# State sums behind the first third's side work, and out_proj two slots later: one change to a two-layer Mamba and expert kernel

## The chip, the cores and the metric

The kernel runs on one core of one Trainium2 chip. A core has a tensor engine (TensorE, PE in the profile), a vector engine (VectorE, DVE), a scalar engine (ScalarE, ACT), a general engine (GpSimd, POOL) and SyncE (SP), which issues most of the DMAs. Each engine has a queue of its own; an instruction waits on semaphores for the results of others. The metric is the time of one execution on the device in microseconds.

## What is computed

The input x is 8 images of 384 channels and 32 x 32 points, 1024 tokens per image. Layer 0 is a Mamba block with an MLP behind it, layer 1 a mixture of four experts with two chosen; both are preceded by a group norm and added to their input. Cut to what matters:

```python
x = x + L0(group_norm(x))
x = x + L1(group_norm(x))

# L0, per image, t = 1024 tokens of 384 channels, layer-normed
xm, z = split(t @ in_proj_w.T)                     # 768 channels each
xc = silu(conv3(xm) + conv_b)
dt, Bm, Cm = split(xc @ x_proj_w.T, [24, 40])
dt = softplus(dt @ dt_proj_w.T + dt_proj_b)
dA = exp(dt * A)                                   # 768 channels x 16 states
h = dA * h + (dt * xc) * Bm                        # scan over the 1024 tokens
y = (sum over states of h * Cm + xc * D) * silu(z)
t = gelu((y @ out_proj_w.T) @ mlp_w1.T + mlp_b1) @ mlp_w2.T + mlp_b2

# L1, per token
coef = weights of the two best of 4 experts
out = sum over e of coef_e * (relu(x @ w1_e.T + b1_e) @ w2_e.T + b2_e)
```

Everything is 32-bit floating point.

## The kernel before

An image is worked in two halves of 512 tokens, so there are 16 halves i. A half has 768 inner channels, six blocks d of 128, and each block has 16 states per channel, done as four groups s of four. A *round* r is one (i, d, s): 24 rounds per half, 384 in all (line 922 on). The 24 rounds of a half are called a block below, counted k = 0 to 23.

A round works on 128 partitions (32 channels x 4 states for each j of four quarters, j = 0 to 3). Its instructions are:

- `drive(r)` (L742, POOL): du = (dt x) times B, 128 x 2048, into one of three buffers du
- `decay(r, j)` (L734, ACT): exp(dt A) for one quarter; quarters 0 and 1 into the PSUM tile da_A, quarters 2 and 3 one after the other into the PSUM tile da_B
- `scan(r, j)` (L750, DVE): the recurrence over 512 tokens, four per round
- `read_out` (L754): h times C, for quarters 0 and 1 on DVE, for 2 and 3 on POOL, both into du
- `sum_states(r)` (L776, PE): four matmuls with the 0/1 matrix `sel` that add the four states into the PSUM tile y of (i, d). It reads what both read_outs wrote, and when it is done du is free for drive(r + 3).
- once in four rounds, when a d is complete, `finish` (L783, DVE): xc = y times silu(z), the gate product; it waits for the last sums of its d. `seed` (L769, ACT) then starts y of the next d with xc times D.

All other work of layer 0 and the first half of the expert layer is *side work*: in_proj for the next half (g_in, L295), x_proj (g_x), the step sizes dt (`delta`: g_dt on PE L396, three activations on ACT L400 to L402, one operation on DVE L404, one on POOL L407, then DMAs that bring dt and dt x back repeated as dtr and dxr), out_proj (g_out, L456), the MLP (hid, L478, and acc, L517), the norms, and the experts' first product (e_hid, L619, results to HBM in r_dram). It is written as generators that yield the engine wanted next, a cost and a number of slots to wait. Three times per round, `side` counts a slot, gives each engine credit (PE 2.7 per slot) and issues ready steps in order of rank while there is credit. This happens while the program is built: the result is a fixed order on each engine. The PE results of side work go to four PSUM banks and are evicted by ACT or DVE in a later slot; the expert lane has the last rank, so it takes what the others leave.

The loop of a round (L922 to L959), in the order in which it is written: `plan`, `sum_states(r - 1)`, `scan(r, 2)`, `drive(r + 1)`, `decay(r, 3)`, side work of the first third, `scan(r, 0)`, `scan(r, 3)`, side work of the second third, `decay(r + 1, 2)`, `scan(r, 1)`, the two read_outs, `decay(r + 1, 0)` and `(r + 1, 1)`, `finish` and `seed` where s = 0, side work of the last third.

out_proj(i) (L445) waits until (i, 5) is in `finished`, which `finish` sets at the end of round k = 0 of the next half, before that round's last side work. It then makes three groups of two times three matmuls; its weights (and those of all lanes) come through rings of three buffers, loaded by SP two ahead. The hidden lane of half i waits for it.

After the loop, what is left of the side work is drained, the routing weights are made, and `experts` runs the second expert product (acc, L1026) over all tokens.

Of the kernel before, what the change touches and what calls it, by code (L numbers as in the profile page):

```python
# [112 lines left out]
def layer0(ctx, tc, io, ident, cmean, eps, dram, x1_dram, gn1, logits, r_dram, group_norm):  # L113
# [77 lines left out]
    def exp_ln_tables():  # L191
        S.preload_act_table_set(EXP_LN_SET)
# [4 lines left out]
    def bank(name):  # L197
        held[0] += 1
        return ps_g.tile([P, T], F32, name=name, tag="g")
# [31 lines left out]
    def statistics(b):  # L231
        st = p2.tile([P, NH * J, 6], F32, name="st")
        for k in range(NH):
            for j in range(J):
                if b == 0:
                    part = xt[k][:, j, :]
                else:
                    yield "-", 0, 3
                    part = pst.tile([P, T], F32, name="part")
                    nc.sync.dma_start(part, chunk_of(io["x"], b * NH + k)[:, j, :])  # L240
                    yield "-", 0, 3
                yield "DVE", 0.7, 0
                V.bn_stats(st[:, k * J + j, :], part)
        g = wp.tile([P, 2], F32, name=f"gn{b}")
        yield from group_norm(st, bank, free, p2, g)

        yield "bank", 0.2, 2
        small = bank("shift")
        PE.matmul(small[:, 0:1], lhsT=cmean, rhs=g[:, 1:2], start=True, stop=True)
        yield "ACT", 0.6, 2  # L250
        mean_w = p1.tile([P, P], F32, name="mean_w")
        S.activation(mean_w, cmean, AF.Identity, scale=g[:, 0:1])
        S.activation(g[:, 1:2], small[:, 0:1], AF.Identity, bias=g[:, 1:2], scale=-float(J))
        free()
        gn[b] = g, mean_w
# [68 lines left out]
    def gate(i, d):  # L324
        while i not in normal or not w_in.turn("in_proj", ND + d):
            yield "-", 0, 1
        yield "bank", 3, 0
        g = in_proj(i, ND + d)
        yield "ACT", 0.6, 2
        z = pz.tile([P, T], F32, name="z")  # L330
        S.copy(z, g)
        free()
        gates[i, d] = z
# [40 lines left out]
    def load_b(i, s):  # L374
        bt[i, s] = load_rows("b", i, s)

    def load_c(i, s):
        ct[i, s] = load_rows("c", i, NS + s)
# [61 lines left out]
    def evict(g, wait, cost, engine, then):  # L440
        yield engine, cost, wait
        then(g)
        free()

    def out_proj(i):  # L445
        while (i, ND - 1) not in finished or i - 1 in tt:
            yield "-", 0, 1
        t = p1.tile([P, J, T], F32, name="tt")
        for j in range(J):
            g = None  # L450
            for k in range(2):
                yield "bank" if k == 0 else "PE", 3, 0
                w = w_out.take("out_proj", 2 * j + k)
                g = bank("g_out") if k == 0 else g
                for d in range(3):
                    PE.matmul(g, lhsT=w[:, d, :], rhs=xc[i, 3 * k + d], start=(k + d == 0), stop=(k == 1 and d == 2))  # L456

            def then(g, j=j):
                S.copy(t[:, j, :], g)
                ready.setdefault(i, []).append(j)  # L460
            begin(evict(g, 2, 0.6, "ACT", then), rank=1)
        out_done.add(i)
        while len(ready.get(i, [])) < J:
            yield "-", 0, 1
        tt[i] = t
# [73 lines left out]
    def out_lane():  # L539
        for i in range(NCH):  # L540
            yield from out_proj(i)
# [13 lines left out]
    def in_order():  # L555
        for n in range(NCH):
            if n > 0:
                yield from (ND + d for d in range(3, 6))
            yield from range(ND)
            yield from (ND + d for d in range(3))  # L560
        yield from (ND + d for d in range(3, 6))
# [161 lines left out]
    def at(r):  # L723
        i, k = divmod(r, per)
        return i, *divmod(k, NG)
# [18 lines left out]
    def scan(r, j):  # L744

        i, d, s = at(r)
        a = da[r, "A"][:, j, :] if j < 2 else da[r, "B"]
        b = du[r][:, j, :]
        start = 0.0 if i % NH == 0 else carry[:, d, j, s:s + 1]
        V.tensor_tensor_scan(a if j < 2 else b, a, b, start, ALU.mult, ALU.add)  # L750
# [20 lines left out]
    def sum_states(r):  # L771
        i, d, s = at(r)
        y, h = yp[i, d], du.pop(r)
        m = P // Q
        for j in range(Q):
            PE.matmul(y[j * m:(j + 1) * m, :], lhsT=sel, rhs=h[:, j, :], start=False, stop=(s == NG - 1),  # L776
                      tile_position=(0, j * m), skip_group_check=True)
# [23 lines left out]
    def begin(*new, rank=2):  # L801
        tasks.extend(Task(t, rank) for t in new)
# [59 lines left out]
    def drain(until=lambda: not tasks):  # L862
        while not until():
            credit.update(PE=99, ACT=99, DVE=99, batch=99)
            issue(everything)
            slot[0] += 1
        credit.update(PE=0, ACT=0, DVE=0)

    with tc.manual_schedule():
        w_in = Stream(pw_in, [("in_proj", k) for k in in_order()])  # L870
        begin(statistics(0))
        drain()
        begin(norm(0))
        drain()
        S.preload_act_table_set(SILU_SET)
        begin(*(conv(0, d, at_once=True) for d in range(ND)), x_proj(0))
        drain(lambda: len(xc) == ND)
        exp_ln_tables()
        drain()
        load_b(0, 0)  # L880
        load_c(0, 0)
        begin(delta(0, 0))
        drain()
        for s in range(1, NG):
            load_b(0, s)
            load_c(0, s)
        begin(delta(0, 1), rank=0)
        begin(*(gate(0, d) for d in range(3)))
        begin(silus(zs, gates, [(0, d) for d in range(3)]))
        begin(norm(1))  # L890
        w_out = Stream(pw_out, [("out_proj", k) for i in range(NCH) for k in range(2 * J)])
        w_1 = Stream(pw_1, [("mlp_w1", u) for i in range(NCH) for u in range(NF)])
        w_2 = Stream(pw_2, [("mlp_w2", 4 * j + 2 * half + k) for i in range(NCH) for half in range(2)
                            for j in range(J) for k in range(2)])
        seed(0, 0)
        w_e = Stream(pw_e, [("e_w1", u) for i in range(NCH) for u in range(E * J)])
        drive(0)
        for j in (2, 0, 1):
            decay(0, j)
        begin(out_lane(), rank=1.5)  # L900
        begin(hidden_lane(), rank=3)
        begin(second_lane(), rank=2.5)
        begin(expert_lane(), rank=4)

        batched = [False]

        def side(*engines, act=None):
            slot[0] += 1
            credit["PE"] = min(credit["PE"] + PE_SLOT, 4)
            credit["DVE"] = min(credit["DVE"] + DVE_SLOT, 2)  # L910
            if act is not None:
                credit["ACT"] = act + min(credit["ACT"], 0)
            issue({e: ENOUGH[e] for e in engines})

        def batch():

            ready = [t for t in tasks if t.engine == "batch" and t.ready <= slot[0]]
            batched[0] = bool(ready) and not batched[0]
            if batched[0]:
                min(ready, key=Task.urgency).resume()  # L920

        for r in range(rounds):  # L922
            i, d, s = at(r)
            k = r % per
            more = r + 1 < rounds
            plan(i, k)
            if r > 0:
                sum_states(r - 1)
            scan(r, 2)
            if more:  # L930
                drive(r + 1)
            decay(r, 3)
            batch()
            act = () if batched[0] else ("ACT",)
            side("PE", "DVE", *act, act=ACT_FIRST)
            scan(r, 0)
            scan(r, 3)
            last_token(G.tensor_copy, r, BB, du[r][:, BB, :])
            side("PE", *act)
            if more:  # L940
                decay(r + 1, 2)
            scan(r, 1)
            read_out(V, r, A, da[r, "A"])
            last_token(V.tensor_copy, r, A, da[r, "A"])
            read_out(G, r, BB, du[r][:, BB, :])
            if more:
                decay(r + 1, 0)
                decay(r + 1, 1)
            if s == 0 and r > 0:
                finish(*at(r - 1)[:2])  # L950
                seed(i, d)
            side("PE", "DVE", "ACT", act=ACT_LAST)
        sum_states(rounds - 1)
        finish(NCH - 1, ND - 1)
        begin(last_x1(), route(), rank=0)
        drain()
# [116 lines left out]
```

## Time and profile before

| | us |
|---|---|
| median of 3 runs | 4095.63 (4087.91 to 4099.21) |
| the profiled execution | 4110.87 |
| its span, first to last instruction | 4109.0 |
| first read_out to last read_out of the rounds | 3325 (82 to 3407) |
| from the end of the rounds to the end | about 690 |
| mean granted TensorE clock | 0.948 |
| blocks of 24 rounds from 670 us on | 210 to 214 each |
| blocks of 24 rounds before that | 192 to 199 each |

The page gives, for each group of instructions, its line, engine, operation, the tiles written and read, the shapes and the count; behind the first bar the time busy in us and the mean of one in ns; behind the second bar how long the engine sat idle just before these instructions, and who ended most of that. "PEld" are weight loads. A view by stretch lists for each stretch its length, then the busy time and number of instructions on PE, PEld, DVE, ACT and POOL, then the granted TensorE clock as a share of full speed, the busy share of the DMA engines, and GB/s. A view of waits lists engine and line, what it waited for, the total in us, how often, and the longest. A timeline lists start, duration, engine, line, operation and tiles, how many instructions are merged into the line, and in brackets the idle time before it and who ended it.

A 32-bit matmul is two instructions in the records: a group of three 128 x 512 products shows as x6, the four matmuls of `sum_states` as x8.

### The profile page before, as it was taken

What the parts mean: (1) busy time and instruction counts of PE and PEld (TensorE: products, weight loads), DVE (VectorE), ACT (ScalarE), POOL (GpSimd) and SP (SyncE); (2) the same over time, 40 slices, a digit from 0 to 9 for tenths busy, and PEclk for the clock granted to TensorE, in tenths of its full rate; (3) what the DMA queues carried; (4) which work ended last, traced back from release to release, by engine and by line L of the source; (5) the groups of instructions that cost most, each with busy time, mean ns of one, the idle gap of its engine ahead of it and who ended that gap; (6) DMA issues with size and microseconds to landing.
All of it is one profiled execution on the core that took longest, in us unless ns stands there. A gap on an engine that the chain in (4) does not pass through costs nothing. (4 is left out here: it accounts for less than half of the span.)

```text
span 4109.0 us, 35186 instructions
## 1 busy us (share of the span) xinstructions
PE 3709.2 (90%) x10294; PEld 1385.4 (34%) x10294; DVE 3032.3 (74%) x3081; ACT 2422.7 (59%) x3762; POOL 2782.5 (68%) x1070
## 2 busy tenths in 40 slices
PE   6678888999999999998999989898999899889999
PEld 2123223333333333333333333333333334334444
DVE  4888888878887878888878787878787781165552
ACT  4657676767686768676766677677767663200000
POOL 3898988788877888888878888888878881000000
PEclk8779898999999999999999999999999999899999
DMA  4444444464545454555455444555554543465552
GB/s 127 134 137 134 152 142 158 143 201 164 172 150 180 164 167 151 192 166 175 154 187 172 159 163 159 181 167 166 165 167 155 163 161 96 169 222 189 185 188 98
DMA packets 372499, 665.31 MB, mean 162 GB/s; under 512 B 40252, under 2 KB 151228, under 8 KB 370132
## 3 DMA queue, kind: packets, MB, share of 16 engines
q1 hardware_dynamic: 342352, 610.02, 45.8%
q10 hardware_dynamic: 29956, 53.05, 3.4%
q8 instruction: 83, 1.36, 0.1%
q14 instruction: 108, 0.88, 0.1%
HBM read 535.90 MB, written 127.01 MB: 161 GB/s over the span
## 5 line engine op out<-in xcount | busy, mean ns | idle before, releaser
L742 POOL TENSOR_TENSOR du<-dxr,b 128x2048 f32<-128x2048 f32 x384 | 1740.9, 4534 | 25.1 <-PE y L776 15.1
L754 POOL TENSOR_TENSOR du<-du,c 128x1024 f32<-128x1024 f32 x384 | 905.8, 2359 | 229.2 <-DVE du L750 199.7
L734 ACT ACTIVATE da_A<-dtr_a,w_a_log 128x512 f32<-128x512 f32 x768 | 527.6, 687 | 280.3 <-DVE du L754 122.1
L734 ACT ACTIVATE da_B<-dtr_b,w_a_log 128x512 f32<-128x512 f32 x768 | 527.3, 687 | 260.4 <-DVE du L750 207.2
L478 PE MATMUL hid<-tt,mlp_w 128*128 128x512 f32 x1152 | 541.5, 613 | 63.8 <-ACT h L482 46.7
L776 PE MATMUL y<-du,sel 128*32 128x512 f32 x3072 | 466.3, 642 | 134.1 <-DVE du L754 92.2
L750 DVE TENSOR_TENSOR_SCAN du<-da_B,carry,du 128x512 f32<-128x512 f32 x384 | 488.4, 1272 | 123.2 <-ACT da_B L734 114.8
L619 PE MATMUL e_hid<-xn,e_w 128*128 128x512 f32 x1080 | 519.2, 627 | 55.4 <-ACT r L623 37.9
L295 PE MATMUL g_in<-xt,in_proj 128*128 128x512 f32 x1152 | 554.7, 619 | 13.8 <-ACT xt L287 7.0
L517 PE MATMUL acc<-h,mlp_w 128*128 128x512 f32 x1152 | 543.4, 614 | 24.5 <-ACT h L493 15.9
L750 DVE TENSOR_TENSOR_SCAN du<-da_B,du 128x512 f32<-128x512 f32 x384 | 464.7, 1210 | 130.5 <-ACT da_B L734 114.0
L1026 PE MATMUL acc<-r,w_e_w 128*128 128x512 f32 x1152 | 496.6, 594 | 13.1 <-DVE r L1023 13.1
L750 DVE TENSOR_TENSOR_SCAN da_A<-da_A,carry,du 128x512 f32<-128x512 f32 x384 | 489.3, 1274 | 9.6 <-ACT da_A L734 9.0
L750 DVE TENSOR_TENSOR_SCAN da_A<-da_A,du 128x512 f32<-128x512 f32 x384 | 465.5, 1212 | 27.0 <-ACT da_A L734 25.0
L754 DVE TENSOR_TENSOR du<-da_A,c 128x1024 f32<-128x1024 f32 x384 | 470.3, 1225 | 13.2
L478 PEld LDWEIGHTS hid<-tt,mlp_w 128*128 128x128 f32 x1152 | 215.8, 193 | 366.5 <-issue 239.1
L517 PEld LDWEIGHTS acc<-h,mlp_w 128*128 128x128 f32 x1152 | 216.6, 195 | 343.9 <-issue 247.7
L295 PEld LDWEIGHTS g_in<-xt,in_proj 128*128 128x128 f32 x1152 | 210.0, 194 | 353.5 <-issue 255.1
L619 PEld LDWEIGHTS e_hid<-xn,e_w 128*128 128x128 f32 x1080 | 207.4, 199 | 356.2 <-issue 250.3
L1026 PEld LDWEIGHTS acc<-r,w_e_w 128*128 128x128 f32 x1152 | 219.6, 191 | 290.1 <-issue 287.3
L456 PE MATMUL g_out<-xc,out_proj 128*128 128x512 f32 x576 | 284.0, 641 | 32.9 <-DVE xc L783 32.9
L407 POOL TENSOR_TENSOR dtx<-dt,xc 128x512 f32<-128x512 f32 x96 | 122.1, 1272 | 217.5 <-DVE dt L404 217.5
(129 smaller groups left out, 3030.2 us busy)
## 6 DMA issues: line engine op xcount, KB each, us to landing
dxr<-dxr_dram SPq DMA_DIRECT2D x384, 256.0 KB, 4.7
mlp_w<-in_mlp_w SPq DMA_DIRECT2D x384, 192.0 KB, 2.9
dtr_b<-dtr_dram SPq DMA_DIRECT2D x192, 256.0 KB, 4.2
dtr_a<-dtr_dram SPq DMA_DIRECT2D x192, 256.0 KB, 3.2
r_dram<-r ACTq DMA_DIRECT2D x192, 256.0 KB, 3.5
r<-r_dram SPq DMA_DIRECT2D x64, 768.0 KB, 4.8
in_proj<-in_in_proj SPq DMA_DIRECT2D x192, 192.0 KB, 4.0
e_w<-in_e_w SPq DMA_DIRECT2D x192, 192.0 KB, 3.2
```

What stands on the lines that cost most here:

```text
L295: PE.matmul(g, lhsT=w[:, j, :], rhs=xt[i][:, j, :], start=(j == 0), stop=(j == J - 1))
L407: G.tensor_tensor(dtx, dt, xc[i, d], ALU.mult)
L456: PE.matmul(g, lhsT=w[:, d, :], rhs=xc[i, 3 * k + d], start=(k + d == 0), stop=(k == 1 and d == 2))
L478: PE.matmul(g, lhsT=w[:, j, :], rhs=tt[i][:, j, :], start=(j == 0), stop=(j == J - 1))
L517: PE.matmul(g, lhsT=w[:, n, :], rhs=hs[mine[n]], start=(k + n == 0), stop=(k == 1 and n == 2))
L619: PE.matmul(h, lhsT=w[:, j, :], rhs=xn[:, j, :], start=(j == 0), stop=(j == J - 1))
L734: S.activation(out, dtr[i, d][pair][:, j % 2, :], AF.Exp, scale=neg_a[:, d, j, s:s + 1])
L742: G.tensor_tensor(du[r], dxr[i, d], wide(bt[i, s].unsqueeze(1), [P, Q, T]), ALU.mult)
L750: V.tensor_tensor_scan(a if j < 2 else b, a, b, start, ALU.mult, ALU.add)
L754: engine.tensor_tensor(du[r][:, js, :], h, wide(ct[i, s].unsqueeze(1), [P, 2, T]), ALU.mult)
L776: PE.matmul(y[j * m:(j + 1) * m, :], lhsT=sel, rhs=h[:, j, :], start=False, stop=(s == NG - 1), tile_position=(0, j * m), skip_group_check ...
L1026: PE.matmul(acc[j], lhsT=e2[:, e, d, j, :], rhs=r[:, d, :], start=(e + d == 0), stop=(e + d == E + J - 2))
```

## The change

Two edits. The sums of the round before are issued behind the first third's side work of a round in place of at its start, so on PE, whose order is the order of issue, that side work stands ahead of them. And out_proj(i) waits two slots more once its half is finished; a round has three.

```diff
     def out_proj(i):
         while (i, ND - 1) not in finished or i - 1 in tt:
             yield "-", 0, 1
+        yield "-", 0, 2
         t = p1.tile([P, J, T], F32, name="tt")
...
             k = r % per
             more = r + 1 < rounds
             plan(i, k)
-            if r > 0:
-                sum_states(r - 1)
             scan(r, 2)
             if more:
                 drive(r + 1)
...
             batch()
             act = () if batched[0] else ("ACT",)
             side("PE", "DVE", *act, act=ACT_FIRST)
+            if r > 0:
+                sum_states(r - 1)
             scan(r, 0)
             scan(r, 3)
```

Lines behind the first edit are numbered one higher in the changed kernel (L777 for the sums, L784 for finish, and so on). Since side work is placed by credit and rank, the second edit also moves other side work: what stands where changes on PE, ACT, DVE, POOL and SP.

## The prediction

> **What bounds the kernel now.** I read the page first, then the busy times by stretch of the 384 rounds, then the waits, then the timeline where the two edits act. The page:
>
> ```profile
> PE 3709.2 (90%) x10294; PEld 1385.4 (34%) x10294; DVE 3032.3 (74%) x3081; ACT 2422.7 (59%) x3762; POOL 2782.5 (68%) x1070
> ...
> L776 PE MATMUL y<-du,sel 128*32 128x512 f32 x3072 | 466.3, 642 | 134.1 <-DVE du L754 92.2
> ...
> L456 PE MATMUL g_out<-xc,out_proj 128*128 128x512 f32 x576 | 284.0, 641 | 32.9 <-DVE xc L783 32.9
> ```
>
> TensorE (PE) is busiest. The two rows that the edits aim at, the state sums (L776) and out_proj (L456), stood behind 134.1 and 32.9 us of idle PE. By stretch (PE, weight loads, DVE, ACT, POOL busy, granted clock), an early block of 24 rounds and two late ones:
>
> ```profile
> 472.00:670.00 198.00, 171.53 (x487) 59.07 (x486) 171.35 (x188) 136.78 (x210) 175.93 (x78) 0.91 0.47 153
> ...
> 1942.00:2154.00 212.00, 194.95 (x584) 71.25 (x584) 170.99 (x155) 156.71 (x248) 171.39 (x56) 0.98 0.50 164
> 2154.00:2368.00 214.00, 198.93 (x558) 72.61 (x558) 172.92 (x188) 145.56 (x223) 176.17 (x78) 0.95 0.52 171
> ```
>
> The early block (198 us) has no engine over 89%: loops of waits set it. Late blocks (213 us; there are twelve) have PE at 92 to 93%: about 17 us idle per block. So the waits of TensorE are worth looking at by place:
>
> ```profile
> PE hid L478 <- ACT h L482: 38.6, 18, 2.8
> PE y L776 <- DVE du L754: 32.4, 24, 5.8
> PE g_out L456 <- DVE xc L783: 30.6, 9, 5.1
> ```
>
> These three lead the answer for 760 to 3390 us. Of the 134.1 us in front of the sums only 32.4 lie in the late 64% of the time, at the ends of blocks. There the sums start, in the median, 4 to 6 us after the two read_outs that they add up (from the start times round by round): TensorE is late, the data are not. What TensorE's lateness costs the others is seen at dt (L400 to L404):
>
> ```profile
> 2193.55 1.06 PE L776 MATMUL y<-du,sel 128*32 128x512 f32 x8
> ...
> 2194.54 1.12 PE L396 MATMUL g_dt<-dbc,w_dt_proj 24*128 24x512 f32 x2
> ...
> 2195.75 0.69 ACT L400 ACTIVATE dt<-g_dt,b 128x512 f32<-128x512 f32 x1 [3.76 <-POOL du L754]
> ...
> 2197.89 0.75 DVE L404 SCALAR_TENSOR_TENSOR dt<-g_dt,w_dt_b,dt 128x512 f32<-128x512 f32 x1 [2.46 <-ACT dt L402]
> ```
>
> Sums, g_dt, then ACT 0.09 us after g_dt's end (the releaser named there had long been done), then DVE: g_dt, once in four rounds, holds up both. In 77 of 96 cases ACT starts within 0.3 us of g_dt's end; DVE idles 159.3 us, 81 times, in front of L404.
>
> **The Trainium skill.** "TensorE: Matmul & The Clock Gate", section Step-by-step: what each phase is for: "The MATMULs themselves stay in program order"; only weight loads go ahead. So ready matmuls behind an unready sum wait with it. The trace agrees: 6.5 us was the longest such wait. Same page, section HAM oscillation: gaps over about 3.4 us bring the array back to half rate. The trace agrees in part: after a gap of 4.71 us the clock is 0.50 from 2155 to 2162 and 0.69 to 2170, but a 3.87 us gap left it low for one window of 3.4 us only. "PSUM — Partial Sum Buffer", section Engine vs sequencer instructions: the other three engines are strict FIFO; so the 3.76 us above hold all that ACT has behind it.
>
> **The change, part by part.** No instruction is added or removed. A sum set is eight instructions in 1.06 us (they overlap), a chunk of six matmul instructions about 2.76 us, or 0.92 per 128x512 product. As built, the sums are moved past 2.26 products on average (77 times none, 199 times three, 38 times four), 2.1 us.
>
> (a) Work of the first third comes 1.06 us earlier against the sums, g_dt most of all. Taking for each of the 77 cases the smallest of 1.06 (plus the wait of the sum in front), ACT's wait and DVE's wait gives 64 us. It counts only where TensorE can follow; it is idle 8% and its idle time in a block's middle comes from late ACT evictions (the L482 row, and 25.6 us for L623 next in that list). I take half: -32, bounds 0 and -64. The early waits of the sums are inside this: 97 us of them lie in rounds 0 to 71, where TensorE has spare time anyway and only the g_dt behind them matters.
>
> (b) out_proj. At rounds 96, 144, ... 336 (six, a new image) it runs into this:
>
> ```profile
> 2145.03 1.10 PE L776 MATMUL y<-du,sel 128*32 128x512 f32 x8 [1.53 <-DVE du L754]
> 2146.06 4.56 PE L456 MATMUL g_out<-xc,out_proj 128*128 128x512 f32 x10
> 2155.33 2.08 PE L456 MATMUL g_out<-xc,out_proj 128*128 128x512 f32 x2 [4.71 <-DVE xc L783]
> 2157.33 1.94 PE L776 MATMUL y<-du,sel 128*32 128x512 f32 x8
> 2159.20 2.07 PE L396 MATMUL g_dt<-dbc,w_dt_proj 24*128 24x512 f32 x2
> ```
>
> Ten of twelve instructions were ready, two wait for finish. With the edit none of the twelve stands there: TensorE would sit idle from the sums of round 23 to the sums of round 0, which need the seed, ready at 2156.7. What fills it is the expert lane. It is last in rank; in the built order it runs one to three chunks behind the present one for most of a block, and at these six places three of its chunks (e_hid 9, 10, 11) now stand in the last round and the first third of the new one, where before it had run dry. Sum from 2131.6, the end of the sums of round 21: acc 2.8, e_hid 2.8, var and sums 3.1 (waiting for read_out 22, at 2140.2), var 1.0, three e_hid 8.3, sums 1.06, g_dt 1.1: 2151.6, then idle to 2156.7. So 5 us idle instead of 6.2, one chunk more done by then, g_dt already done. Worth 2.8 us plus what half rate no longer costs (7 x 0.5 + 8 x 0.31 = 6.0 us now): bounds 0 and -9, I take -4 each, -24.
> At rounds 72, 120, ... 360 (seven, second half of an image) the waits are 1.90, 1.22 and 0.34 us and the clock stays at 1.00. Two e_hid chunks go two rounds ahead, none stands at the boundary; by the same sum about 4 us of idle in one piece. If the clock drops it costs up to 6; I take +1 each, +7 (bounds 0 and +42).
>
> (c) Sums later. First, drive (L742) needs the buffer of the third round back. From the end of the sums to drive's start the median is 4.6 us, the lowest 5% under 0.4; taking off what the sums are moved past, 80 drives would start later, by 104 us together. POOL covers it: it idles 199.7 us in front of L754 and 150.7 in front of L759, both for DVE scans that come later than drive's end. dtx, carry copy and read_out queue behind drive; DVE's scan needs it only a round on. I take +10, bounds 0 and +104. Second, finish (L783) needs the last sums of its four rounds: 35 of 95 would wait, 46 us; the scan, the seed and ACT's last third queue behind it. But g_dt comes 5 to 7 us later on TensorE and holds ACT up anyway in the next round. I take +9, bounds 0 and +46.
>
> (d) After the loop three products more are left (749.6 against 746.6): +2.8. The tail from 3416 to 4109 is otherwise the same instructions; out_proj's two slots pass there without time. ACT's xn normalising moves from round 0, where it lay beside a 4.35 us wait for dtr_a, to round 1 at the six places: 2.4 us, paid from the 4.02 us that ACT waited there for g_dt: nothing. If g_dt is not early there, it costs up to 6 x 2.4. out_proj's and the experts' weight loads move on SP with their chunks; two loads ahead cover them.
>
> Sum: -32 - 24 + 7 + 10 + 9 + 3 = -27 us. The profiled execution took 4110.87 us (span 4109.0), so 4084; it lies 15 us above the median of the runs, and on that median, 4095.63, the forecast is 4068.
>
> **Rivals.** *Nothing comes of it*: TensorE's 92% is the bound and what is saved at g_dt is waited for at the next bank. For it: idle PE is spread over a dozen places per block. Against: these are waits for ACT, which (a) makes earlier. 4096. *All of it*: (a) and (b) at their full ends, -64 - 54 with the same costs: 4006. *Slower, by the ring of three du buffers*: each late sum holds drive, POOL passes it to its read_out, and that to the next drive and to DVE. POOL's cover is 350 us over 384 rounds, 0.9 a round; the 80 late drives are 1.3 us late on average and come in PE-heavy rounds one behind the other. It decides once a drive is some 2 us later than now, the mean shift of the sums. With 90 of the 104 us passed on and the rest as taken: 80 more than the forecast, 4149; with half of them, 52 in place of 10, 4111. For it: drive's row on the page has 15.1 us of waiting for the sums already, 13 times. Against: POOL waits for scans in nearly every round.
>
> **How the numbers follow.** The measurement tells 0.3%, 12 us. Forecast's neighbourhood (4035 to 4083) 0.49, all of it 0.10, nothing 0.18, slower 0.23. Faster 0.59, within 0.3% 0.18, slower 0.23. The range reaches from the all-of-it case to half of the slower one, with some room: 4003 to 4124; the forecast's own is 4035 to 4083.
>
> **What would show it.** Right: the wait in front of L404 falls from 159.3 us to near 100; idle before the sums falls below 60 us in rounds 0 to 71 and below 20 from 760 us on, apart from waits for the seed; g_out's wait for xc is gone; a late block takes 209 to 211 us in place of 213. Wrong: drive's idle for the sums rises from 15 to 80 us or more while L754's does not fall; or the clock in the blocks that begin at 72, 120, ... drops below 0.95, half rate at every boundary.

## The result, and the profile after

The changed kernel took 4117.72 us (median of 7 runs, 4106.95 to 4123.26), the kernel before 4097.01 us on the same chip (7 runs, 4087.91 to 4108.82): a ratio of 1.0044, 95% interval 1.0028 to 1.0060. It is slower by 0.4%, more than the 0.3% that count here as a difference. The forecast was 4068; the time lies inside the range, on the wrong side of before. The profiled execution took 4123.26 us (span 4121.5, mean granted clock 0.938; before 4110.87, 4109.0 and 0.948).

From the page of after, the busy line and three rows (after each second bar: idle time of the engine just before, and what ended it):

```profile
PE 3709.5 (90%) x10294; PEld 1401.0 (34%) x10294; DVE 3025.4 (73%) x3081; ACT 2424.7 (59%) x3762; POOL 2783.2 (68%) x1070
...
L743 POOL TENSOR_TENSOR du<-dxr,b 128x2048 f32<-128x2048 f32 x384 | 1740.0, 4531 | 243.2 <-PE y L777 228.2
...
L777 PE MATMUL y<-du,sel 128*32 128x512 f32 x3072 | 466.1, 638 | 134.6 <-ACT y L770 67.0
...
L457 PE MATMUL g_out<-xc,out_proj 128*128 128x512 f32 x576 | 266.3, 618 | 0.0
```

The work is the same to 0.3 us on TensorE. out_proj's wait for xc is gone, as aimed at. The idle time in front of the sums is as large as before, but its largest part is now a wait for the seed. New is the drive: 228.2 us of waiting for sums, 15.1 before. Two rows further down, in the list of groups:

```profile
L404 DVE SCALAR_TENSOR_TENSOR dt<-g_dt,w_dt_b,dt 128x512 f32<-128x512 f32 x96 | 71.7, 747 | 72.6 <-ACT dt L402 72.6
...
L784 DVE TENSOR_TENSOR xc<-y,z 128x512 f32<-128x512 f32 x96 | 65.9, 687 | 226.5 <-PE y L777 226.5
```

DVE's wait for dt fell from 159.3 to 72.6 us, further than forecast; finish's wait for the last sums of its d rose to 226.5 us (57 of 96 times), from 17.2 (9 times). The early and the two late stretches that the prediction showed:

```profile
472.00:670.00 198.00, 169.53 (x488) 59.55 (x488) 170.76 (x187) 136.62 (x210) 175.63 (x78) 0.90 0.46 153
1942.00:2154.00 212.00, 193.14 (x564) 71.86 (x564) 172.60 (x157) 154.32 (x244) 172.37 (x55) 0.94 0.50 165
2154.00:2368.00 214.00, 198.62 (x566) 73.99 (x565) 167.26 (x182) 145.78 (x223) 171.39 (x78) 0.95 0.50 164
```

In the second stretch the clock fell from 0.98 to 0.94 and 564 matmul instructions were done in place of 584. (The stretches are fixed times, and after lies a few us later in its rounds there.) Measured from the first DVE read_out of a half to the first of the next, the twelve late blocks take 2563 us together, 2544 before: those of odd halves 209 to 211, as forecast for all, those of even halves 215 to 220. How the 19 us are shared out between even and odd halves depends on where the cut between two halves is put; the sum hardly does.

Both kernels were laid over each other round by round, from the start of one DVE read_out to that of the next (halves 4 to 13). The largest single loss is in the first round of an even half: it takes 5.7 us longer than before, behind a step that is 3.2 us shorter. This is that place in the timeline of after (start, duration, engine, line, operation; idle time before it and who ended it in brackets; SPq marks transfers issued by SyncE):

```profile
2148.08 4.66 SPq L388 DMA_DIRECT2D dxr<-dxr_dram  x4
2148.44 2.36 POOL L755 TENSOR_TENSOR du<-du,c 128x1024 f32<-128x1024 f32 x1 [1.38 <-DVE du L751]
...
2150.19 5.31 PE L620 MATMUL e_hid<-xn,e_w 128*128 128x512 f32 x12
...
2152.83 1.39 SPq L217 DMA_DIRECT2D e_w<-in_e_w  x2
...
2158.29 4.51 PE L620 MATMUL e_hid<-xn,e_w 128*128 128x512 f32 x6 [2.79 <-DMA e_w<-in_e_w]
2162.73 1.06 PE L777 MATMUL y<-du,sel 128*32 128x512 f32 x8
...
2163.86 0.69 DVE L784 TENSOR_TENSOR xc<-y,z 128x512 f32<-128x512 f32 x1 [6.85 <-PE y L777]
2163.91 4.54 POOL L743 TENSOR_TENSOR du<-dxr,b 128x2048 f32<-128x2048 f32 x1 [6.07 <-PE y L777]
2164.59 0.69 ACT L770 ACTIVATE y<-xc,w_d_skip 128x512 f32<-128x512 f32 x1 [5.94 <-DVE xc L784]
```

The sums at 2162.73 are those of the last round of a half; the later of the two read_outs that they add up is the POOL line at 2148.44, which ends at 2150.80. In front of them stand the three expert chunks that the prediction counted on as filler. The weights of the third come 2.79 us late: their load (the first of the two at 2152.83) stands in SyncE's queue behind four loads of dxr, whose issue took until 2152.74. After that pause the chunk runs 4.51 us, where it took 2.74 us at full rate. DVE waits 6.85 us for the sums, POOL 6.07, ACT 5.94: three engines stand still for one chunk of the lane that has the last rank. It is not the only such place: over halves 4 to 13 finish waits 5.6 us on average at k = 0 of even halves and 5.5 at k = 4, and in odd halves 3.5 us at k = 4 and 5.1 at k = 12.

### The profile page after: what moved, and what is told of

Read it like the earlier page. It is cut to its first block, busy times and chain, and to the rows that moved or that the text cites. A ratio compares the mean times of both kernels' runs of the same rounds, so it can differ in the third digit from the quotient of the medians.

```text
span 4121.5 us, 35221 instructions
## 1 busy us (share of the span) xinstructions
PE 3709.5 (90%) x10294; PEld 1401.0 (34%) x10294; DVE 3025.4 (73%) x3081; ACT 2424.7 (59%) x3762; POOL 2783.2 (68%) x1070
## 5 line engine op out<-in xcount | busy, mean ns | idle before, releaser
L743 POOL TENSOR_TENSOR du<-dxr,b 128x2048 f32<-128x2048 f32 x384 | 1740.0, 4531 | 243.2 <-PE y L777 228.2
L755 POOL TENSOR_TENSOR du<-du,c 128x1024 f32<-128x1024 f32 x384 | 906.3, 2360 | 139.4 <-DVE du L751 112.5
L295 PE MATMUL g_in<-xt,in_proj 128*128 128x512 f32 x1152 | 566.0, 633 | 68.4 <-DMA in_proj<-in_in_proj 38.1
L777 PE MATMUL y<-du,sel 128*32 128x512 f32 x3072 | 466.1, 638 | 134.6 <-ACT y L770 67.0
L620 PE MATMUL e_hid<-xn,e_w 128*128 128x512 f32 x1080 | 508.6, 619 | 53.0 <-DMA e_w<-in_e_w 19.1
L755 DVE TENSOR_TENSOR du<-da_A,c 128x1024 f32<-128x1024 f32 x384 | 470.2, 1225 | 13.2
L295 PEld LDWEIGHTS g_in<-xt,in_proj 128*128 128x128 f32 x1152 | 221.2, 200 | 401.6 <-issue 276.3
L457 PE MATMUL g_out<-xc,out_proj 128*128 128x512 f32 x576 | 266.3, 618 | 0.0
L1024 DVE TENSOR_TENSOR r<-r,spread 128x1536 f32<-128x1536 f32 x64 | 112.3, 1755 | 190.3 <-DMA r<-r_dram 174.8
```

What stands on the lines that cost most here:

```text
L295: PE.matmul(g, lhsT=w[:, j, :], rhs=xt[i][:, j, :], start=(j == 0), stop=(j == J - 1))
L620: PE.matmul(h, lhsT=w[:, j, :], rhs=xn[:, j, :], start=(j == 0), stop=(j == J - 1))
L743: G.tensor_tensor(du[r], dxr[i, d], wide(bt[i, s].unsqueeze(1), [P, Q, T]), ALU.mult)
L755: engine.tensor_tensor(du[r][:, js, :], h, wide(ct[i, s].unsqueeze(1), [P, 2, T]), ALU.mult)
L1024: V.tensor_tensor(r4, r4, wide(spread[i][:, :, e, :].unsqueeze(1), [P, J, TT, P]), ALU.mult)
```

## The experiments

Twelve more kernels were timed on three chips, each against the kernel before on its own chip. Ratios are of medians to that kernel, with 95% intervals; 0.01 is 41 us. The state sums of round r - 1 are issued in round r, which belongs to s = r mod 4. Where s = 1, that third holds g_dt as a rule, and the sums are the first of a new d, which need the seed; where s = 0, they are the last of a d, for which finish waits.

| kernel | ratio | interval | finish | L404 | drive |
|---|---|---|---|---|---|
| after: both edits | 1.0044 | 1.0028 to 1.0060 | 226 | 73 | 243 |
| e1: sums late | 0.9883 | 0.9867 to 0.9899 | 82 | 88 | 119 |
| e2: out_proj late | 1.0066 | 1.0050 to 1.0081 | 52 | 162 | 71 |
| e3: both, sums first where s = 0 | 0.9912 | 0.9899 to 0.9925 | 69 | 109 | 134 |
| e4: sums late where s = 1 only | 0.9881 | 0.9865 to 0.9898 | 19 | 96 | 26 |
| e5: sums late where s = 0 only | 1.0014 | 1.0004 to 1.0024 | 63 | 151 | 70 |
| e6: out_proj late in halves 0 to 2 only | 1.0053 | 1.0040 to 1.0067 | 42 | 156 | 65 |
| e7: both, sums first in round k = 0 | 0.9938 | 0.9926 to 0.9951 | 173 | 72 | 193 |
| e8: both, sums first where s = 0, k > 0 | 0.9963 | 0.9950 to 0.9975 | 87 | 106 | 141 |
| e9: sums late where s is not 0 | 0.9872 | 0.9853 to 0.9892 | 32 | 101 | 93 |
| e10: e9, out_proj late from half 3 on | 0.9885 | 0.9865 to 0.9904 | 56 | 106 | 118 |
| e11: ACT's dt step one slot later | 1.0018 | 1.0010 to 1.0027 | 33 | 164 | 62 |
| e12: e11, and sums late where s = 1 | 0.9922 | 0.9908 to 0.9936 | 26 | 171 | 125 |

The last three columns are idle us of DVE in front of finish, of DVE in front of L404 and of POOL in front of drive, from each profiled execution (before: 17, 159, 25).

**The two edits one by one (e1, e2).** The diff is the one shown above, one edit at a time.

> The first edit alone: sums behind the first third in every round, out_proj as before. Theory F (finish): the loss comes from finish, whose DVE wait for the sums rose from 17 to 227 us, so this is slower than before by 0.3 to 0.8%, with 150 us or more of DVE idle in front of finish. Theory O (out_proj): the loss is the second edit's, so this is 0.3 to 1% faster than before. Theory R (ring): slower like F, but with drive's idle for the sums above 200 us deciding.

> The second edit alone: out_proj two slots later, sums at the start of the round. F and R: g_out's 33 us of waiting are gone, finish waits about 17 us as before, time within 0.3% of before or up to 0.7% faster. O: 0.4% slower, with more half-rate time than the 429 us of before.

Late sums alone gain 1.2%, 48 us; out_proj's two slots alone cost 0.7%, 27 us. This is the side of theory O, and both are larger than it had them; time at half rate (granted clock 0.50) is 361 us in e1 and 521 in e2. Together the edits would have come to -21 us; the full change lost 18 (0.44% of 4097). So some 39 us are lost only where both edits act. (Each ratio is known to about 6 us, so this difference of three to some 11.)

**Which late sums gain (e4, e5).** Only the rounds named are moved:

```diff
-            if r > 0:
+            if r > 0 and s != 1:      # e5: s != 0
                 sum_states(r - 1)
...
             side("PE", "DVE", *act, act=ACT_FIRST)
+            if r > 0 and s == 1:      # e5: s == 0
+                sum_states(r - 1)
```

> The kernel before, with the sums behind the first third only in rounds with s = 1, the ones with g_dt. This is the prediction's part (a) by itself. F: faster than before by 0.5 to 1%, DVE's wait in front of L404 falls from 159 to 80 to 110 us, finish waits about as before. If TensorE's own work is the bound: same as before within 0.3%, with the L404 wait lower and other waits higher.

> The kernel before, with the sums behind the first third only in rounds with s = 0, the ones whose finish needs them; out_proj as before. Theory I (interaction: late sums hurt at finish only when out_proj's delay has put more work in front of them): within 0.3% of before, finish waits 40 to 90 us. Theory F (late sums at finish hurt by themselves): slower by 0.5 to 1.2%, as much as the changed kernel lost against the one that keeps finish's sums first.

The rounds with s = 1 hold the whole gain of edit 1 (0.9881 against 0.9883), more than the 1% expected. Late sums for finish, alone, cost next to nothing, as theory I had it: 0.14%, whose interval leaves out zero but lies within the 0.3%. DVE does wait 63 us for them there; with out_proj in its old place that wait decides nothing.

Where in time e4 gains tells by which way. Of the 96 instructions L404, 91 stand between DVE's read_out of a round with s = 1 and that of the next, s = 2. From the start of the one read_out to the start of the other, these steps take 78 us less in e4 than before, all 96 together; the other steps together take 17 us more. In e1 the same steps take 89 us less. In them DVE's wait in front of L404 falls from 149 to 86 us in e4. (These are profiled executions, and that of before lies 14 us above the median of its runs.) The rows, before and e4:

```profile
L404 DVE SCALAR_TENSOR_TENSOR dt<-g_dt,w_dt_b,dt 128x512 f32<-128x512 f32 x96 | 72.0, 750 | 159.3 <-ACT dt L402 159.3
```

```profile
L404 DVE SCALAR_TENSOR_TENSOR dt<-g_dt,w_dt_b,dt 128x512 f32<-128x512 f32 x96 | 71.7, 746 | 96.4 <-ACT dt L402 96.4
```

So the gain lies where g_dt, ACT's dt step and L404 follow each other, as part (a) of the prediction had it.

**What the full change loses by finish (e3, e7, e8).** To the full change:

```diff
+            if r > 0 and s == 0:      # e7: k == 0; e8: s == 0 and k > 0
+                sum_states(r - 1)
             scan(r, 2)
...
-            if r > 0:
+            if r > 0 and s != 0:      # e7: k != 0; e8: s != 0 or k == 0
                 sum_states(r - 1)
```

> The changed kernel, but in rounds with s = 0, whose finish needs the sums, they stay at the start of the round. F: DVE's wait at finish falls from 227 to under 50 us, the wait in front of L404 stays under 110, and the time falls below before, to a ratio of 0.985 to 0.997 against before. R: three of four drives still wait, drive's idle stays above 150 us, and the ratio stays at 1.003 or more. O: no better than the changed kernel, 1.004.

> The changed kernel, but in round 0 of each half the sums stay at the start of the round, ahead of the expert chunk that out_proj's delay has brought there. If that chunk in front of the last finish of a half is what costs: finish's wait at k = 0 (5.8 us in every second half) goes, time falls by 25 to 40 us to a ratio of 0.995 to 0.999. If the loss is spread over all six finishes of a half: 5 to 12 us less than the changed kernel, ratio 1.001 to 1.003.

> The complement: the changed kernel with the sums at the start of the round where s = 0, except in round 0 of a half. If round 0 is what costs: 15 to 25 us less than the changed kernel, ratio 0.998 to 1.001. If the loss is spread over the finishes: 40 to 50 us less, ratio 0.992 to 0.995, near the kernel that keeps the sums first for all finishes (0.991).

With finish's sums first again, and both edits otherwise as they were, the kernel is 0.9% faster than before: 54 us come back. Round 0 of a half alone, one finish in six, brings 43 us, a little more than expected, and the five others alone 33, between the two expectations; they overlap, since their sum is more than both together. Four kernels make a square, with the other sums late in all of them. With out_proj in its old place, finish's sums first (e9) or late (e1) give 0.9872 and 0.9883; with out_proj later (e3, after), 0.9912 and 1.0044. Late sums for finish cost 0.1% in the one case and 1.3% in the other. From the list of waits of e3 over the whole span (us in total, times, longest us):

```profile
POOL du L743 <- PE y L777: 108.9, 52, 5.9
...
DVE xc L784 <- PE y L777: 69.3, 38, 9.1
...
DVE du L751 <- POOL du L743: 25.6, 14, 16.3
```

Finish waits 69 us in place of 226, not under 50 as expected. Two things speak against the ring of three du buffers as the cause: the drive still waits 109 us in a fast kernel, and DVE's scans, which need what drive writes, wait for it 25.6 us in e3 and 25.6 us in the full change too (13 times there), 15.9 before. Round by round, the first round of an even half takes 1.0 us longer than before in e3, 5.7 in the full change. Over all rounds, the steps that hold finish, from the read_out of a round with s = 0 to the next, take 133 us longer in the full change than in e1; all others take 60 us less.

Why the edits cost more together than apart is read from how far behind TensorE is. From the end of DVE's read_out to the start of the sums, for the last sums of a d (median of 96): 4.0 us before, 5.4 in e1, 4.6 in e2, 8.5 with both, 5.4 in e3. The number of products in front of these sums does not tell it: between one set of sums and the next, where the next is finish's, stand 6.9 in e1 and 8.3 with both, but 9.8 in e5, where finish waits 63 us (mean of halves 4 to 13, counted in the traces). At k = 0 of an even half the timeline shows what holds the sums up: filler in the place that out_proj left, which waits for its own weights. What puts TensorE behind at the other five finishes was not traced.

**Where out_proj's slots cost (e6, e10, e9).**

```diff
         while (i, ND - 1) not in finished or i - 1 in tt:
             yield "-", 0, 1
+        if i < 3:                     # e10: i >= 3
+            yield "-", 0, 2
```

e9 is e10 without this edit: the sums are late except where s = 0, out_proj is where it was. out_proj of half i stands at the start of half i + 1, so e6 moves it at rounds 24, 48 and 72.

> The kernel before, with out_proj's two slots in the first three halves alone. If the two slots cost only where the expert lane has nothing yet to fill the gap with (it starts in round 87): slower than before by 12 to 18 us, ratio 1.003 to 1.0045, round 72 reached 12 to 16 us later. If they cost at every block's end: 3/16 of 27 us, 5 us, ratio about 1.001.

> Sums behind the first third except where s = 0, out_proj as before: the sums' side of the kernel that keeps finish's sums first, without the second edit. If late sums away from finish cost nothing beyond what g_dt gains: ratio 0.986 to 0.990, level with the two kernels at 0.988; finish waits under 25 us. If late sums in rounds with s = 2 and 3 cost by the ring: 0.991 or more, drive's idle above 80 us.

> The same, with out_proj's two slots only from half 3 on, where the expert lane runs. If the second edit costs only in the first three halves: level with the kernel without it, ratio 0.985 to 0.990, and 8 to 16 us below the kernel that has the two slots everywhere (4061.76 us). If it costs at each half: 0.990 to 0.992.

The two slots in the first three halves alone cost 0.53% of the 0.66%, 22 of 27 us and more than the 12 to 18 expected. The rest lies within the intervals. There the expert lane has not begun (it starts near round 87), so nothing fills the place. TensorE at the start of the third half, before:

```profile
466.70 1.22 PE L776 MATMUL y<-du,sel 128*32 128x512 f32 x8
467.85 4.56 PE L456 MATMUL g_out<-xc,out_proj 128*128 128x512 f32 x10
473.36 1.12 PE L456 MATMUL g_out<-xc,out_proj 128*128 128x512 f32 x2 [0.95 <-DVE xc L783]
474.82 1.06 PE L776 MATMUL y<-du,sel 128*32 128x512 f32 x8 [0.34 <-ACT y L769]
475.82 1.12 PE L396 MATMUL g_dt<-dbc,w_dt_proj 24*128 24x512 f32 x2
476.87 5.42 PE L456 MATMUL g_out<-xc,out_proj 128*128 128x512 f32 x12
482.22 1.06 PE L776 MATMUL y<-du,sel 128*32 128x512 f32 x8
```

and in e6:

```profile
469.56 1.06 PE L778 MATMUL y<-du,sel 128*32 128x512 f32 x8
477.73 1.93 PE L778 MATMUL y<-du,sel 128*32 128x512 f32 x8 [7.10 <-ACT y L771]
479.59 2.07 PE L396 MATMUL g_dt<-dbc,w_dt_proj 24*128 24x512 f32 x2
481.59 10.42 PE L458 MATMUL g_out<-xc,out_proj 128*128 128x512 f32 x18
```

Before, TensorE stood 1.3 us and did twelve instructions of out_proj in this gap. In e6 it stands 7.10 us. Then sums and g_dt take nearly twice as long, and 18 instructions of out_proj stand in front of the next sums in place of 12. Counted from the start of the first line, g_dt ends after 12.1 us in place of 10.2, and the next sums start after 22.4 us (at 491.94) in place of 15.5: 6.9 us are lost at this one boundary. From half 3 on, where expert chunks are at hand, e10 against e9 shows no difference outside the intervals.

e9 is the fastest that was run, 4044.28 us against 4098 before. Against e1 and e4 it is not told apart: the intervals overlap. Finish waits 32 us in it and the drive 93, more than the 25 and 80 named, at no cost that shows.

**Is it g_dt that gains (e11, e12)?** The prediction priced edit 1 by the waits from g_dt to ACT and on to DVE. e11 takes ACT's wait away with nothing moved on TensorE; e12 adds late sums where s = 1.

```diff
     def delta(i, d):
...
         projected.add((i, d))
-        yield "ACT", 2.0, 1
+        yield "ACT", 2.0, 2
```

> The kernel before with nothing moved but dt's three activations on ACT, which wait two slots behind g_dt and not one. If what the late sums gain is ACT's and DVE's wait for g_dt: ACT no longer stands at L400, DVE's wait in front of L404 falls below 80 us, ratio 0.984 to 0.993. If the gain of the late sums is another one (TensorE's own order): within 0.3% of before.

> The sums late only in the rounds with s = 1, where g_dt stands, as in e4, on top of e11's step of ACT one slot later. In e11 ACT no longer stood at L400 (1.2 us in place of 251.8) and its dt step began 2.8 us behind g_dt's end in the median, so g_dt 1.06 us earlier can be felt by nobody there. If e4's gain goes by g_dt to ACT and DVE: nothing to gain here, ratio 0.999 to 1.004, as e11's 1.0018. If it goes by the other side work of that third on TensorE (products and their banks a set of sums earlier): most of e4's 1.2% is there again, ratio 0.988 to 0.993, with the wait in front of L404 still near 160 us.

e11 decides nothing. In it ACT waited for g_dt once in 96 times, 1.2 us in all (252 us of idle time in front of L400 before), but its dt step began 2.8 us behind g_dt, and DVE then waited for ACT's three activations: L404's wait stayed at 164 us, and nothing was gained. In e12, on top of e11, late sums gain 39 us (1.0018 to 0.9922), about four fifths of the 49 us that e4 gains over before, though there was no wait for g_dt to shorten. The rows of the list of groups, e11:

```profile
L776 PE MATMUL y<-du,sel 128*32 128x512 f32 x3072 | 453.0, 645 | 147.6 <-DVE du L754 88.2 <-ACT y L769 44.5 <-DVE carry L759 14.9
...
L404 DVE SCALAR_TENSOR_TENSOR dt<-g_dt,w_dt_b,dt 128x512 f32<-128x512 f32 x96 | 71.8, 748 | 163.6 <-ACT dt L402 163.5
```

and e12:

```profile
L776 PE MATMUL y<-du,sel 128*32 128x512 f32 x3072 | 451.9, 641 | 120.3 <-DVE du L754 101.1 <-ACT y L769 17.7 <-POOL du L754 1.4
...
L404 DVE SCALAR_TENSOR_TENSOR dt<-g_dt,w_dt_b,dt 128x512 f32<-128x512 f32 x96 | 72.1, 751 | 171.1 <-ACT dt L402 171.1
```

TensorE's wait in front of the first sums of a d became shorter, of which the seed's part fell from 44.5 to 17.7 us. Added up for those sums alone, whoever ended the wait, it is 59 us in e11 and 18 in e12, 39 before and 7 in e4. So late sums can gain without g_dt: ready products pass sums that wait for their seed.

This is not how e4 gains, though. Before, 37 of the 39 us lie in rounds 0 to 71, where e4 is only 11 us shorter. From round 96 on they are 1.7 us, and e4 is 48 us shorter there. In e11 they are 21 us from round 96 on: the later dt step had made waits of its own, and e12 takes part of them away. And e12 gains in other places: against e11 the steps that hold L404 are only 19 of 44 us shorter, and its wait in them is not (157 us, 149 in e11). How much of e12's gain is this idle time was not isolated.

## Why the prediction was wrong, point by point

**The step that failed is (b), out_proj's two slots, -24 + 7, and with it the sum, which added the edits as if they did not meet.** Forecast and result lie 45 us apart (-27 and +18). (b) alone cost +27 us in place of -17, 44 us; with late sums it cost some 39 more, for which the sum had nothing; the other parts gained about 38 us more than forecast (-48 alone in place of -10). Three things in (b) were wrong.

- The boundaries at rounds 24 and 48 were not priced at all, and the one at 72 with +1: the sum began at round 96 (even) and 72 (odd). Slots at these three alone cost 22 of the 27 us (e6). The edit leaves a place empty, and what fills it has to be there in every half. At the later boundaries the forecast gain did not come: e2's trace is 17 us behind before at round 96 and 15 at the last round. In the full change most of the loss lies later: against e1 it is 10 us at round 96 and 74 at the last round.
- At the even boundaries the sum let three expert chunks run one behind the other in 8.3 us and had the sums of round 23 follow in time; "two loads ahead cover them" was said of their weights. With both edits the third chunk's weights came 2.79 us late at 2158.29 (their load stood behind those of dxr), the chunk took 4.51 us in place of 2.74, and the sums ended near 2163.8. With the sums at the start of the round (e2) the third chunk stands behind those sums, and its weights, 0.70 us late there, hold up no finish. So the filler was the one that the prediction named; that the late sums put it in front of what finish, drive and the seed wait for was not priced.
- At the odd boundaries +1 each stood for about 4 us of idle time in place of 3.5. In e2 it is 6.65 us in one piece, and half rate behind it. What this costs there was not separated from the rest of e2:

```profile
2376.05 1.36 PE L777 MATMUL y<-du,sel 128*32 128x512 f32 x8 [0.69 <-DVE du L755]
...
2384.56 1.93 PE L777 MATMUL y<-du,sel 128*32 128x512 f32 x8 [6.65 <-ACT y L770]
2386.42 2.07 PE L396 MATMUL g_dt<-dbc,w_dt_proj 24*128 24x512 f32 x2
2388.42 6.07 PE L457 MATMUL g_out<-xc,out_proj 128*128 128x512 f32 x8
```

**Part (c), finish, +9 (46 us of waiting).** Alone it was near: DVE waits 82 us in e1 with 17 before, 65 more where 46 were worked out, and e5 shows +0.14%, 6 us, for it. In the sum it was wrong, because it was worked out from where before's sums stood, with out_proj in its old place: 226 us of waiting in the full change, and e3 gets 54 us of time back by it. Drive, +10 of 104: its wait rose by 94 us in e1 (119 less 25), as worked out, at no visible cost; e1 and e4, with 119 and 26 us, take the same time.

**Part (a), -32.** The way was the one named, and the size too small: 48 us, in the rounds that were named (e4), within the bounds 0 and -64. The step that was off is "I take half", because TensorE was 92% busy. It could follow further than that: from round 96 on its idle time fell from 194 us before to 166 in e4, 13 us of it in front of hid (L478), one of the late evictions that the prediction had counted on. The early waits of the sums were rightly written off, as shown above. The sentence cited from the Trainium skill, "TensorE: Matmul & The Clock Gate", section Step-by-step: what each phase is for, that "The MATMULs themselves stay in program order", carried this argument both ways: for edit 1, where g_dt passes a set of sums of 1.06 us, and against the pair, where a sum that is ready stands behind a product that is not. The trace agrees: at 2158.29 above, sums whose data had been ready at 2150.80 start behind the late chunk. (The 6.5 us named as the longest such wait is the longest but for the very first sums, which waited 14.8 us.)

**Part (d), +2.8 after the loop.** From the last read_out to the end: 701.9 us before, 702.1 after. Nothing to be seen.

**The rivals.** The slower case was right about the side and named another mechanism: the ring of du buffers. The drive's wait, its sign, came out plainly (228 us, over the 80 named). But POOL's waits for DVE's scans in front of its read_out and its carry copy (L754 and L759, in after L755 and L760) fell as the drive's rose, from 350 to 207 us, DVE waited for drive no longer in the full change than in e3, and e1 and e3 are fast with 106 and 109 us of the drive's wait. A fourth du buffer, which would have tested it by itself, was not tried: there is no room for it in the on-chip memory as the kernel uses it. The clock's part is real and not the whole: time at half rate rose from 429 to 511 us, but e3 has 479 and gains. "Nothing comes of it" fails by e1 and e4: TensorE at 92% left room for 1.2%.

## What to carry to other kernels

On an engine whose queue keeps its order, the order should follow who waits. An instruction that others wait for (g_dt where s = 1, the last sums of a d where s = 0) should have nothing in front of it that nobody needs yet or that is able to wait itself: low-rank filler brings its own late weights with it. Sort the instances of one instruction by these two cases, and move them apart (here the sums late where s = 1, first where s = 0), rather than all together. Two edits to one queue are priced in the order that both give, from the first pass of the loop on, and the fill-in phase is priced by itself. And when a test takes a wait away by moving an instruction, look first whether it made other waits (e11); where the time was gained, step by step, told more here than the totals.

## What the runs showed of the hardware

TensorE's lower rate came with shorter pauses too than the prediction took. Of 35 stretches with a low granted clock (0.50) between 700 and 3300 us in the trace of before, 22 are single windows of 3.4 us, and the longest pause of TensorE near them (from 6 us before to 4 us behind their start) is 1.8 to 2.8 us. But of 44 pauses of 1.8 to 2.9 us there, only 23 have such a stretch near them, so the length of the pause alone does not decide. The five pauses of 4.5 us and more all had a stretch of 10 to 14 us. So "TensorE: Matmul & The Clock Gate", section HAM oscillation, with its 3.4 us, holds here for the long pauses and not for the short ones. In a long pause the clock falls before it is over: at 2379.56, 1.7 us into the 6.65 us of e2 above.

What half rate costs is seen in e6 above: behind a pause of 7.10 us the eight instructions of a set of sums took 1.93 us in place of 1.06, g_dt 2.07 in place of 1.12, and 18 instructions of out_proj, with the low clock for about half of that time, 10.42 us, 579 ns each, against 5.42 for 12 before, 452 each.
